# Expert results added to the residual stream in DRAM by accumulating scatters, instead of rows of z that are gathered up and added later

## The chip, the cores and the metric

The kernel runs on one core of one Trainium2 chip. The metric is device time in microseconds (us). Before the change it is 1237.41 us, the median of three runs (1237.15 to 1238.29). The core's engines are named as in the profile: PE multiplies matrices (PEld loads its weights), DVE and ACT work on vectors, POOL works on vectors more slowly and issues the indirect transfers, SP issues plain transfers. The queues of SP, ACT and POOL are each worked in order, and all their transfers run on the same 16 DMA engines.

## What is computed

Two layers act on a residual stream `x` of 3327 rows of 256 floats. Each layer is a graph step and a mixture of experts, both on the normalized stream, both added to it:

```python
x = x + gnn0(layernorm(x), adj)     # mean over neighbours (adj == 1), then a 256x256 matrix
x = x + ffn0(layernorm(x))          # 16 experts 256->512->256 with silu gate, top 2 per row
x = x + gnn1(layernorm(x), adj)     # attention over neighbours (adj != 0), leaky relu
x = x + ffn1(layernorm(x))          # 6 experts 256->256->256->256 with relu, top 2 per row
```

In both mixtures a row's result is the weighted sum over its two best experts, so that each row of `x` gets two added rows per layer. The two experts of one row always differ.

## The kernel before, in words

**Tiles.** Rows are cut into 26 tiles of 128 (the last has 127 rows, N = 3327, NP = 3328). `xs` holds the whole residual stream in SBUF, 128 partitions x 26 tiles x 256. Tiles form chunks of four, and chunks form the blocks of the graph step: 3, 2, 1 and 1 chunks.

**Graph step** (`graph`, L416). For each block, all 26 source tiles are streamed: `load_mask` (L373) loads a piece of the transposed adjacency on SP (three buffers) and DVE turns it into a 0/1 mask (L390), and PE multiplies it with `y`, the prepared rows (L475). In the first block `prepare` is called for one group of tiles after another just ahead of its use: groups of 1, 1, 2, then 4 tiles. `prepare0` (L515) loads `x` into `xs` on SP. `prepare1` (L673) first has to bring the first layer's expert results into `xs`. Both then normalize (`norm`, L173, whose power is taken on POOL at L183) and write `y`. A finished block goes through `finish` (L423): `update` adds the result to `xs`, `norm` gives `h`, SP stores `h` to `hd` in DRAM (L439), and `after` computes the routing. `dispatch` (L192) writes for each row and each of its two experts an entry of three words to the expert's list in DRAM, by a scatter on POOL (L265): where the result is to go, which row of `hd` to read, and the weight.

**Experts.** An expert's list is worked in slots: 67 slots of 128 rows in layer 0, 31 of 256 rows in layer 1. SP loads the slot's list entries (`places`, L320, tile `who`), POOL gathers the rows from `hd` (`rows_in`, L328, one indirect transfer per 128 rows), PE turns them and multiplies (L626, L641 in layer 0, L737, L747 in layer 1), DVE applies bias and weight (L643, L750, L752), and POOL scatters the rows (`rows_out`, L350). The slots are software pipelined by hand: in layer 1 the gathers of slot s + 3 are issued ahead of the scatters of slot s - 1, in layer 0 those of s + 2. The weights of an expert are loaded on SP when a slot begins another expert. Slots are not full: the lists are first filled with idle entries (tile `idle`, L165) whose target lies out of bounds, and the scatter leaves such rows out.

**The results.** A scatter goes to `zd`, which has two rows of 256 for every row of `x`, one for each of its two experts. No two scatters write the same row, so `zd` is declared as disjoint views (L94) and no scatter waits for another. `results` (L362) loads z for a chunk on SP. In layer 1's `prepare1` the two z rows are added on POOL (on DVE for the first chunk, L678) and the sum is added to `xs` on DVE (L679). At the end of the kernel all z is loaded again, added to `xs` on DVE (L777) and stored from ACT's queue (L779, and L784 for the 127 rows of the last tile).

Halfway through layer 0's experts ACT's queue packs the weights of layer 1's experts into one DRAM array, `w1d`, by transfers from DRAM to DRAM (`pack1`, L604).

Of the kernel before, what the change touches and what calls it, by code (L numbers as in the profile page):

```python
# [9 lines left out]
F32 = mybir.dt.float32  # L10
I32 = mybir.dt.int32
# [4 lines left out]
OP = mybir.AluOpType  # L16
# [3 lines left out]
P = 128  # L20
# [5 lines left out]
def kernel(  # L26
# [26 lines left out]
    nc = tc.nc  # L53
    N, D = x.shape
    E0, _, H0 = ffn0_w1.shape
# [18 lines left out]
    SLOTS0 = (2 * N - E0) // P + E0  # L74
    S1 = 2 * P
    SLOTS1 = (2 * N - E1) // S1 + E1
    FAR = 1 << 20
# [12 lines left out]
        dram.tile([E * NP + 2 * P, 3], I32, name=f"list{i}") for i, E in enumerate((E0, E1))  # L90
    ]
    views = [dram_disjoint_views(li[:, :], 2 * NT) for li in lists]
    zd = dram.tile([2 * NP, D], F32, name="zd")
    zviews = dram_disjoint_views(zd[:, :], max(SLOTS0, 2 * SLOTS1))  # L94
    def row_bc(v, name):
        n = v.shape[0]
        t = const.tile([P, n], F32, name=name)
# [36 lines left out]
    slot_p1 = slot_numbers("slot_p1", S1, 3)  # L134

    where = const.tile([P, NT, 2, 3], I32, name="where")
    nc.gpsimd.iota(where, pattern=[[2 * P, NT], [1, 2], [0, 3]], base=0, channel_multiplier=2)
    nc.gpsimd.iota(where[:, :, :, 1], pattern=[[P, NT], [0, 2]], base=0, channel_multiplier=1)
    where_w = where.bitcast(F32)[:, :, :, 2]

    none = const.tile([P, 1], F32, name="none")
# [6 lines left out]
    def operands():  # L148

        small["w0"] = by_chunk(gnn0_wt, "w0t"), row_bc(gnn0_wt[DL, :], "w0r")  # L150
        small["w1"] = by_chunk(gnn1_w, "w1t"), row_bc(gnn1_w[DL, :], "w1r")
        small["gw"], small["gb"] = by_chunk(gate_w, "gw"), row_bc(gate_b, "gb")
        small["a"] = row_bc(gnn1_a[D:], "a_bc")
        small["rw1"] = by_chunk(router_w1, "rw1")
        small["rb1"] = const.tile([P, 1], F32, name="rb1")
        nc.scalar.dma_start(small["rb1"], router_b1.rearrange("(p o) -> p o", o=1))
        small["rw2"] = const.tile([P, E1], F32, name="rw2")
        nc.scalar.dma_start(small["rw2"], router_w2)
        small["rb2"] = row_bc(router_b2, "rb2")
        for li in lists:  # L160
            nc.scalar.dma_start(li.rearrange("(p c) w -> p c w", p=P), idle[:, : li.shape[0] // P, :])
        if N < NP:
            nc.scalar.dma_start(zd[2 * N :, :], zrow[: 2 * (NP - N), :])

    idle = const.tile([P, (E0 * NP + 2 * P) // P, 3], I32, name="idle")  # L165
    nc.gpsimd.memset(idle, 0)
    nc.gpsimd.memset(idle[:, :, 0], FAR)
    zrow = const.tile([2, D], F32, name="zrow")
    nc.gpsimd.memset(zrow, 0.0)

    last = {}
# [175 lines left out]
        nc.scalar.copy(xT, ps)  # L347
        return xT

    def rows_out(s, who, y):  # L350
        n = who.shape[1]
        for h in range(n):
            nc.gpsimd.indirect_dma_start(  # L353
                out=zviews[n * s + h], out_offset=bass.IndirectOffsetOnAxis(ap=who[:, h, 0:1], axis=0),
                in_=y[:, h, :], in_offset=None, bounds_check=2 * NP - 1, oob_is_err=False,
            )

    def weight(who, h):

        return who.bitcast(F32)[:, h, 2:3]  # L360

    def results(blk, zp):  # L362

        n, t0 = len(blk), blk[0]
        z = zp.tile([P, BT, 2, D], F32, name="z")
        nc.sync.dma_start(z[:, :n], zd[2 * t0 * P : 2 * (t0 + n) * P, :].rearrange("(t p k) d -> p t k d", p=P, k=2))
        return z

# [47 lines left out]
    def graph(name, prepare, value, op, wx, update, after, steps, between=None):  # L416
        with ExitStack() as st:
# [5 lines left out]
            def finish(blk, aT):  # L423

                n, t0 = len(blk), blk[0]
                for i, t in enumerate(blk):
                    r = rows(t)
                    ps = ps_mm.tile([P, D + 1], F32, name="mm")
                    for k in range(KD):
                        nc.tensor.matmul(ps[:r], aT[:, k, i * P : i * P + r], wx[:, k, :],  # L430
                                         start=(k == 0), stop=(k == KD - 1))
                    rden = work.tile([P, 1], F32, name="rden", bufs=4)
                    nc.vector.reciprocal(rden[:r], ps[:r, D:])
                    update(t, r, ps, rden)
# [12 lines left out]
                yield  # L447
                yield from after(blk, hT)
# [3 lines left out]
            for b, block in enumerate(GRAPH):  # L452
# [30 lines left out]
                parts = []  # L483
# [153 lines left out]
    def out0(s, who, hid):  # L637
        w3 = w0[s % 2][2]
        ps = ps_acc.tile([P, 512], F32, name="acc")
        for c in range(NC0):  # L640
            nc.tensor.matmul(ps[:, :D], hid[:, c, :], w3[:, c // 2, c % 2, :], start=(c == 0), stop=(c == NC0 - 1))  # L641
        y = io.tile([P, 1, D], F32, name="y")
        nc.vector.tensor_scalar(y[:, 0, :], ps[:, :D], weight(who, 0), None, op0=OP.mult)  # L643
        rows_out(s, who, y)

    who, xg, xT, hid, which = {}, {}, {}, {}, {}
    for s in range(-3, SLOTS0 + 1):
# [19 lines left out]
    stage.close()  # L667


    stage = ctx.enter_context(ExitStack())  # L670
    zp = stage.enter_context(tc.tile_pool(name="zp", bufs=2))

    def prepare1(y, g):  # L673
        n = len(g)
        z = results(g, zp)
        for i, t in enumerate(g):
            adder = nc.vector if t < BT else nc.gpsimd
            adder.tensor_tensor(z[:, i, 0, :], z[:, i, 0, :], z[:, i, 1, :], op=OP.add)  # L678
            nc.vector.tensor_tensor(xs[:, t, :], xs[:, t, :], z[:, i, 0, :], op=OP.add)  # L679
        h = norm(g)  # L680
        er = work.tile([P, BT], F32, name="er")
        for i in range(n):
            prod = work.tile([P, D], F32, name="er_prod", bufs=1)
            nc.vector.scalar_tensor_tensor(prod, h[:, i, :], 1.0, wx["a"], op0=OP.mult, op1=OP.mult,
                                           accum_out=er[:, i : i + 1])
        w = work.tile([P, BT], F32, name="w")
        nc.scalar.activation(w[:, :n], er[:, :n], AF.Exp, bias=wx["c"])
        cols = y[:, g[0] : g[-1] + 1, :, :]
        nc.scalar.copy(cols[:, :, 0, DL], w[:, :n])
        nc.vector.tensor_tensor(cols[:, :, 1, DL], w[:, :n], cols[:, :, 0, DL].bitcast(F32), op=OP.subtract)  # L690
        for i, t in enumerate(g):
            nc.scalar.activation(y[:, t, 0, :DL], h[:, i, :DL], AF.Copy, scale=w[:, i : i + 1])  # L692
            nc.vector.scalar_tensor_tensor(y[:, t, 1, :DL], h[:, i, :DL], w[:, i : i + 1],
                                           y[:, t, 0, :DL].bitcast(F32), op0=OP.mult, op1=OP.subtract)
# [20 lines left out]
        yield  # L715

    graph("1", prepare1, 0.0, OP.not_equal, wx[1], update1, after1, 8)
    stage.close()


    NC1 = H1 // P
# [20 lines left out]
    def out1(s, who, h2):  # L742
# [10 lines left out]
        rows_out(s, who, y)  # L753

    who, xg, xT, h1, h2 = {}, {}, {}, {}, {}
    for s in range(-4, SLOTS1 + 1):
# [12 lines left out]
        if 0 <= s + 2 < SLOTS1:  # L769
            xT[s + 2] = turned(xg.pop(s + 2))  # L770

    tail = ctx.enter_context(tc.tile_pool(name="tail", bufs=len(CHUNKS)))
    zs = [results(blk, tail) for blk in CHUNKS]
    for blk, z in zip(CHUNKS, zs):
        for i, t in enumerate(blk):
            for k in range(2):
                nc.vector.tensor_tensor(xs[:, t, :], xs[:, t, :], z[:, i, k, :], op=OP.add)  # L777
# [42 lines left out]
```

## Time and profile before

| | |
|---|---|
| median of three runs | 1237.41 us |
| profiled execution, its own time | 1231.33 us |
| its span, first to last instruction | 1229.5 us |
| PE busy | 1011.1 us (82%) |
| DVE busy | 457.8 us (37%) |
| ACT busy | 273.3 us (22%) |
| POOL busy | 419.2 us (34%) |
| layer 0: graph / experts, about | 12 to 281 / 292 to 703 us |
| layer 1: graph / experts, about | 703 to 994 / 994 to 1193 us |
| sum of z, store of the result | 1193 to 1229.5 us |
| HBM read, written | 263.18 MB, 33.69 MB |

The page's slices cut the span into 40 equal parts of 30.7 us and give the busy share of each engine in tenths. The chain that ended last is read backwards from the last instruction: each step is what released the one after it. A group of instructions has its busy time, the mean of one, and the idle time of the engine just before it with what ended that. In a row of the timeline the square brackets give the idle time ahead of the instruction and its releaser. "To landing" is the time from a transfer's issue to its completion.

### The profile page before, as it was taken

How to read it: one execution, taken by the hardware profiler on the slowest of the kernel's cores; microseconds unless marked ns; L12 is line 12 of the kernel's file. 1: busy time of each engine (PE TensorE's matmuls, PEld its weight loads, DVE VectorE, ACT ScalarE, POOL GpSimd, SP SyncE). 2: the span in 40 equal slices, each digit the busy share in tenths (PEclk: the TensorE clock that was granted, in tenths of full speed). 3: DMA queues.
4: the chain of work that ended last, by engine and by line, in shares of the span. 5: the costliest groups of instructions: out<-in, count | busy, mean ns of one | idle time of the engine just before them, and what ended most of it. 6: DMA issues, size and time to landing. Idle time of an engine off the chain costs nothing. (4 is left out here: it accounts for less than half of the span.)

```text
span 1229.5 us, 18090 instructions
## 1 busy us (share of the span) xinstructions
PE 1011.1 (82%) x5644; PEld 868.0 (71%) x5644; DVE 457.8 (37%) x1527; ACT 273.3 (22%) x580; POOL 419.2 (34%) x436
## 2 busy tenths in 40 slices
PE   5989979643959999999999768999598429999960
PEld 4768756523959999999999746877476218888850
DVE  5555634532211212212122189666165222222215
ACT  2312012011101111111111133231131204444420
POOL 2000323522322333333333252102333355676730
PEclk9989989875989999999999979999799659999995
DMA  8977653235595655666454057975452044645627
GB/s 301 329 264 260 202 188 105 61 106 193 159 287 158 197 187 192 192 198 199 157 188 108 23 205 267 306 277 177 126 156 71 26 127 139 231 130 167 183 69 292
DMA packets 110572, 221.37 MB, mean 180 GB/s; under 512 B 33390, under 2 KB 55408, under 8 KB 110476
## 3 DMA queue, kind: packets, MB, share of 16 engines
q1 hardware_dynamic: 84240, 178.59, 43.5%
q0 software_dynamic: 15712, 30.73, 9.0%
q10 hardware_dynamic: 10524, 10.89, 2.9%
q8 instruction: 45, 0.74, 0.2%
q14 instruction: 51, 0.42, 0.1%
HBM read 263.18 MB, written 33.69 MB: 241 GB/s over the span
## 5 line engine op out<-in xcount | busy, mean ns | idle before, releaser
L475 PE MATMUL acc<-big,y 128*128 128x512 f32 (+3 forms) x1248 | 305.8, 394 | 42.2 <-ACT y L692 18.7
L475 PEld LDWEIGHTS acc<-big,y 128*128 128x128 f32 (+1 forms) x1248 | 228.5, 197 | 99.6 <-ACT y L692 19.9
L626 PE MATMUL mm<-xT,w 128*128 128x128 f32 x2144 | 266.5, 283 | 14.9 <-ACT xT L347 14.9
L626 PEld LDWEIGHTS mm<-xT,w 128*128 128x128 f32 x2144 | 261.3, 199 | 15.1 <-ACT xT L347 15.1
L353 POOL DMA_INDIRECT zd<-y,who x129 | 128.5, 996 | 264.2 <-DVE y L643 221.6
L265 POOL DMA_INDIRECT list<-where,t_idx x104 | 108.7, 1045 | 203.6 <-DVE t_idx L262 48.4
L333 POOL DMA_INDIRECT xg<-hd,who x129 | 125.7, 974 | 93.7 <-issue 39.0
L634 DVE TENSOR_TENSOR hid<-hid,mm 128x512 f32<-128x512 f32 x67 | 46.0, 687 | 266.5 <-PE mm L626 251.4
L390 DVE TENSOR_SCALAR big<-adj 128x1536 fp32r<-128x1536 int32 (+5 forms) x112 | 107.9, 966 | 95.5 <-PE acc L475 70.1
L641 PE MATMUL acc<-w,hid 128*128 128x256 f32 x536 | 126.6, 379 | 0.0
L188 ACT ACTIVATE ln_h<-xs,ln_nmr,ln_rstd 128x256 f32<-128x256 f32 x104 | 54.4, 591 | 246.0 <-DVE ln_nmr L185 231.7
L641 PEld LDWEIGHTS acc<-w,hid 128*128 128x128 f32 x536 | 96.7, 190 | 10.4
L347 ACT COPY xT<-mm 128x256 f32<-128x256 f32 (+1 forms) x98 | 43.1, 440 | 273.7 <-PE mm L345 248.8
L183 POOL TENSOR_TENSOR ln_rstd<-ln_rstd,half 128x4 f32<-128x4 f32 (+2 forms) x32 | 31.9, 999 | 184.4 <-DVE ln_rstd L182 94.1
L738 ACT ACTIVATE h<-mm,v 128x256 f32<-128x256 f32 x124 | 58.7, 473 | 100.3 <-PE mm L737 100.3
L750 DVE TENSOR_TENSOR y<-acc,v 128x512 f32<-128x512 f32 x31 | 21.4, 691 | 155.6 <-PE acc L747 155.6
L445 PE MATMUL mm<-ident,ln_h 128*128 128x128 f32 x104 | 24.3, 351 | 63.3 <-ACT ln_h L188 63.1
L345 PE MATMUL mm<-ident,xg 128*128 128x128 f32 x258 | 47.7, 286 | 33.8 <-DMA xg<-hd,who 33.8
L345 PEld LDWEIGHTS mm<-ident,xg 128*128 128x128 f32 x258 | 45.7, 199 | 40.5 <-issue 30.0
L737 PE MATMUL mm<-xT,v 128*128 128x256 f32 x248 | 65.9, 389 | 0.7 <-ACT xT L347 0.7
L737 PE MATMUL mm<-h,v 128*128 128x256 f32 x248 | 64.1, 380 | 1.3 <-ACT h L738 1.1
L445 PEld LDWEIGHTS mm<-ident,ln_h 128*128 128x128 f32 x104 | 14.9, 169 | 70.4 <-ACT ln_h L188 69.4
(158 smaller groups left out, 940.4 us busy)
## 6 DMA issues: line engine op xcount, KB each, us to landing
w<-in_ffn_w SPq DMA_DIRECT2D x201, 512.0 KB
adj<-in_adj_t SPq DMA_DIRECT2D x50, 768.0 KB
adj<-in_adj_t SPq DMA_DIRECT2D x36, 1024.0 KB
v<-w1d SPq DMA_DIRECT2D x31, 898.0 KB
z<-zd SPq DMA_DIRECT2D x11, 1024.0 KB
hd<-ln_h SPq DMA_DIRECT2D x12, 512.0 KB
adj<-in_adj_t SPq DMA_DIRECT2D x12, 510.0 KB
w1d<-in_ffn_w ACTq DMA_DIRECT2D x3, 1536.0 KB
```

The lines of the kernel that those rows point to most:

```text
L188: last["h"] = nc.scalar.activation(h[:, i, :], xs[:, t, :], AF.Identity, bias=nmr[:, i : i + 1], scale=rstd[:, i : i + 1])
L265: nc.gpsimd.indirect_dma_start(out=rows_of[2 * (t0 + j) + i], out_offset=bass.IndirectOffsetOnAxis(ap=idx[:, i, j : j + 1], axis=0), in_=w ...
L333: nc.gpsimd.indirect_dma_start(out=xg[:, h, :], out_offset=None, in_=hd, in_offset=bass.IndirectOffsetOnAxis(ap=who[:, h, 1:2], axis=0),)
L345: nc.tensor.transpose(ps[:, k, h * P : (h + 1) * P], xg[:, h, k:D:KD], ident)
L353: nc.gpsimd.indirect_dma_start(out=zviews[n * s + h], out_offset=bass.IndirectOffsetOnAxis(ap=who[:, h, 0:1], axis=0), in_=y[:, h, :], in_ ...
L390: nc.vector.tensor_scalar(mask[:kr, :, :cols], a[:kr, :, :cols], value, None, op0=op)
L475: nc.tensor.matmul(acc[c][k][:, :w], y[:kr, j, part, k * P : (k + 1) * P], mask[:kr, jj, i0 : i0 + w], start=(j == 0 and part == 0), stop= ...
L626: nc.tensor.matmul(q[:, c, :], w[:, k, h0 : h0 + 2 * P - 1 : 2], xT[:, k, :], start=(k == 0), stop=(k == KD - 1))
L634: nc.vector.tensor_mul(hid, hid, ps[1])
L641: nc.tensor.matmul(ps[:, :D], hid[:, c, :], w3[:, c // 2, c % 2, :], start=(c == 0), stop=(c == NC0 - 1))
L737: nc.tensor.matmul(ps[:, c, :], w[:, k, c : H1 : NC1], src[:, k, :], start=(k == 0), stop=(k == 1))
L738: nc.scalar.activation(dst[:, c, :], ps[:, c, :], AF.Relu, bias=w1s[s % 3][:, BB + 2 * i + c : BB + 2 * i + c + 1])
```

## The change

`zd` is gone. A new DRAM array `xd` holds the residual stream, NP rows and 256 rows more. After each graph step's update, SP stores the chunk of `xs` to `xd` (`store`, just ahead of the store of `h`). Each expert slot adds its rows to `xd` by a scatter with an add as its compute operation. The list entry's target is now the row itself, the same for both experts. Since two slots can now add to the same row, a slot's scatters wait until those of the slot before have landed; only the two scatters of one slot in layer 1 are declared free of each other. An idle entry can't be left out by its bounds: it points to one of the 256 spare rows, distinct within a slot. `prepare1` loads `xs` from `xd` in one plain load per group, and there is nothing to add. At the end the result is copied from `xd` to the output by four transfers from DRAM to DRAM, in turn on SP and ACT.

```diff
-    zd = dram.tile([2 * NP, D], F32, name="zd")
-    zviews = dram_disjoint_views(zd[:, :], max(SLOTS0, 2 * SLOTS1))
+    xd = dram.tile([NP + S1, D], F32, name="xd")
...
-    nc.gpsimd.iota(where, pattern=[[2 * P, NT], [1, 2], [0, 3]], base=0, channel_multiplier=2)
-    nc.gpsimd.iota(where[:, :, :, 1], pattern=[[P, NT], [0, 2]], base=0, channel_multiplier=1)
+    nc.gpsimd.iota(where, pattern=[[P, NT], [0, 2], [0, 3]], base=0, channel_multiplier=1)
...
-            nc.scalar.dma_start(zd[2 * N :, :], zrow[: 2 * (NP - N), :])
+            nc.scalar.dma_start(xd[N:NP, :], zrow[: NP - N, :])
+        for h in range(S1 // P):
+            nc.scalar.dma_start(xd[NP + h * P : NP + (h + 1) * P, :], zrow)
...
-    idle = const.tile([P, (E0 * NP + 2 * P) // P, 3], I32, name="idle")
-    nc.gpsimd.memset(idle, 0)
-    nc.gpsimd.memset(idle[:, :, 0], FAR)
-    zrow = const.tile([2, D], F32, name="zrow")
+    idle = {}
+    for i, li in enumerate(lists):
+        n = li.shape[0] // P
+        idle[n] = const.tile([P, n, 3], I32, name=f"idle{i}")
+        nc.gpsimd.memset(idle[n], 0)
+        at = idle[n][:, :, 0]
+        nc.gpsimd.iota(at, pattern=[[1, n]], base=0, channel_multiplier=n)
+        nc.vector.tensor_scalar(at, at, S1 - 1, None, op0=OP.bitwise_and)
+        nc.vector.tensor_scalar(at, at, NP, None, op0=OP.add)
+    zrow = const.tile([P, D], F32, name="zrow")
...
-    def rows_out(s, who, y):
-        n = who.shape[1]
-        for h in range(n):
-            nc.gpsimd.indirect_dma_start(
-                out=zviews[n * s + h], out_offset=bass.IndirectOffsetOnAxis(ap=who[:, h, 0:1], axis=0),
-                in_=y[:, h, :], in_offset=None, bounds_check=2 * NP - 1, oob_is_err=False,
-            )
+    def rows_out(who, y):
+        those = []
+        for h in range(who.shape[1]):
+            ins = nc.gpsimd.indirect_dma_start(
+                out=xd[:, :], out_offset=bass.IndirectOffsetOnAxis(ap=who[:, h, 0:1], axis=0),
+                in_=y[:, h, :], in_offset=None, compute_op=OP.add,
+            ).ins
+            for other in those:
+                tc.declare_no_dep(ins, other, reason="no row twice in a slot")
+            those.append(ins)
...
-    def results(blk, zp):
+    def stream(blk):
         n, t0 = len(blk), blk[0]
-        z = zp.tile([P, BT, 2, D], F32, name="z")
-        nc.sync.dma_start(z[:, :n], zd[2 * t0 * P : 2 * (t0 + n) * P, :].rearrange("(t p k) d -> p t k d", p=P, k=2))
-        return z
+        return xd[t0 * P : (t0 + n) * P, :].rearrange("(t p) d -> p t d", p=P), xs[:, t0 : t0 + n, :]
...
+    def store(blk):
+        to, x_ = stream([t for t in blk if t < NF])
+        nc.sync.dma_start(to, x_)
+        if blk[-1] >= NF:
+            nc.sync.dma_start(xd[NF * P : N, :], xs[: N - NF * P, NF, :])
...
                 h = norm(blk)
+                store(blk)
                 nc.sync.dma_start(hd[t0 * P : (t0 + n) * P, :].rearrange("(t p) d -> p t d", p=P), h[:, :n, :])
...
     def prepare1(y, g):
         n = len(g)
-        z = results(g, zp)
-        for i, t in enumerate(g):
-            adder = nc.vector if t < BT else nc.gpsimd
-            adder.tensor_tensor(z[:, i, 0, :], z[:, i, 0, :], z[:, i, 1, :], op=OP.add)
-            nc.vector.tensor_tensor(xs[:, t, :], xs[:, t, :], z[:, i, 0, :], op=OP.add)
+        of, x_ = stream(g)
+        nc.sync.dma_start(x_, of)
         h = norm(g)
...
-    tail = ctx.enter_context(tc.tile_pool(name="tail", bufs=len(CHUNKS)))
-    zs = [results(blk, tail) for blk in CHUNKS]
-    for blk, z in zip(CHUNKS, zs):
-        for i, t in enumerate(blk):
-            for k in range(2):
-                nc.vector.tensor_tensor(xs[:, t, :], xs[:, t, :], z[:, i, k, :], op=OP.add)
-        full = [t for t in blk if t < NF]
-        nc.scalar.dma_start(
-            out[full[0] * P : (full[-1] + 1) * P, :].rearrange("(t p) d -> p t d", p=P),
-            xs[:, full[0] : full[-1] + 1, :],
-        )
-        if blk[-1] >= NF:
-            nc.scalar.dma_start(out[NF * P :, :], xs[: N - NF * P, NF, :])
+    parts = 4
+    of, to = (a.rearrange("n d -> (n d)").rearrange("(q p f) -> q p f", q=parts, p=N * D // N // parts)
+              for a in (xd[:N, :], out))
+    for q in range(parts):
+        (nc.sync, nc.scalar)[q % 2].dma_start(to[q], of[q])
```

More of the change, by code (lines that the diff above doesn't have):

```diff
@@ L160, in operands @@
         for li in lists:
-            nc.scalar.dma_start(li.rearrange("(p c) w -> p c w", p=P), idle[:, : li.shape[0] // P, :])
+            nc.scalar.dma_start(li.rearrange("(p c) w -> p c w", p=P), idle[li.shape[0] // P])
         if N < NP:
-            nc.scalar.dma_start(zd[2 * N :, :], zrow[: 2 * (NP - N), :])
-    idle = const.tile([P, (E0 * NP + 2 * P) // P, 3], I32, name="idle")
-    nc.gpsimd.memset(idle, 0)
-    nc.gpsimd.memset(idle[:, :, 0], FAR)
-    zrow = const.tile([2, D], F32, name="zrow")
+            nc.scalar.dma_start(xd[N:NP, :], zrow[: NP - N, :])
[11 more added lines that the diff above has]
+    zrow = const.tile([P, D], F32, name="zrow")
     nc.gpsimd.memset(zrow, 0.0)
@@ L643, in out0 @@
         nc.vector.tensor_scalar(y[:, 0, :], ps[:, :D], weight(who, 0), None, op0=OP.mult)
-        rows_out(s, who, y)
+        rows_out(who, y)
     who, xg, xT, hid, which = {}, {}, {}, {}, {}
@@ L667 @@
     stage.close()
-    stage = ctx.enter_context(ExitStack())
-    zp = stage.enter_context(tc.tile_pool(name="zp", bufs=2))
     def prepare1(y, g):
         n = len(g)
-        z = results(g, zp)
-        for i, t in enumerate(g):
-            adder = nc.vector if t < BT else nc.gpsimd
-            adder.tensor_tensor(z[:, i, 0, :], z[:, i, 0, :], z[:, i, 1, :], op=OP.add)
-            nc.vector.tensor_tensor(xs[:, t, :], xs[:, t, :], z[:, i, 0, :], op=OP.add)
+        of, x_ = stream(g)
+        nc.sync.dma_start(x_, of)
         h = norm(g)
@@ L717 @@
     graph("1", prepare1, 0.0, OP.not_equal, wx[1], update1, after1, 8)
-    stage.close()
     NC1 = H1 // P
@@ L752, in out1 @@
             nc.vector.tensor_scalar(y[:, h, :], y[:, h, :], weight(who, h), None, op0=OP.mult)
-        rows_out(s, who, y)
+        rows_out(who, y)
     who, xg, xT, h1, h2 = {}, {}, {}, {}, {}
```

## The prediction, made before the result was known

> **What bounds the kernel now.** I read the page's busy table and slices first, then the chain that ended last, then busy time by windows at the stages that the change touches, and last the POOL rows of the expert loops.
>
> ```profile
> span 1229.5 us, 18090 instructions
> PE   5989979643959999999999768999598429999960
> POOL 2000323522322333333333252102333355676730
> ```
>
> PE is near full from slice 9 to 21 (layer 0's experts) and 34 to 38 (layer 1's). The holes are the ends of stages: slice 22 to 24 (start of layer 1's graph) and the last one. POOL is at half or more in layer 1's experts. The end of the chain, in order of time (start, length, what):
>
> ```profile
> 1189.79 0.97 POOL zd L353
> 1190.76 0.30 POOLq L816
> 1191.07 2.12 DMA zd<-y,who
> 1193.25 5.28 DMA z<-zd
> 1198.54 17.41 DMA z<-zd
> 1215.98 3.77 DVE xs L777 x11
> ```
>
> From the last scatter's landing at 1193.2 everything to 1229.5 is tail: 36.3 us. Busy time by windows (PE, PEld, DVE, ACT, POOL, then granted clock, DMA share, GB/s) shows how it is spent:
>
> ```profile
> 1206.00:1210.00 4.00, 0.00 (x0) 0.00 (x0) 3.40 (x12) 0.00 (x0) 0.00 (x0) 0.50 1.07 401
> 1222.00:1226.00 4.00, 0.00 (x0) 0.00 (x0) 0.00 (x0) 0.00 (x0) 0.00 (x0) 0.50 0.06 19
> 1226.00:1229.50 3.50, 0.00 (x0) 0.00 (x0) 0.00 (x0) 0.00 (x0) 0.00 (x0) 0.50 0.04 15
> ```
>
> The DMA engines are full with 6.8 MB of z and the stores behind it until about 1221. Then one engine in sixteen (share 0.06) works for 6 us: the last store, the 127 rows of tile 25. The start of layer 1's graph, by windows and by PE's waits in its first block:
>
> ```profile
> 712.00:760.00 48.00, 37.29 (x134) 28.68 (x135) 43.11 (x121) 15.53 (x38) 22.16 (x24) 0.86 0.68 233
> ```
>
> ```profile
> PE acc L475 <- ACT y L692: 18.7, 3, 12.1
> PE acc L475 <- DVE big L390: 2.6, 1, 2.6
> ```
>
> DVE is busy 43.1 of 48 us, PE idles 10.7, and most of that is waiting for y, which waits for z and its adds. The scatters, as groups (busy, mean ns | idle before, ended by) and as rows of layer 1:
>
> ```profile
> L353 POOL DMA_INDIRECT zd<-y,who x129 | 128.5, 996 | 264.2 <-DVE y L643 221.6
> L333 POOL DMA_INDIRECT xg<-hd,who x129 | 125.7, 974 | 93.7 <-issue 39.0
> ```
>
> ```profile
> 1029.40 1.01 POOL L353 DMA_INDIRECT zd<-y,who  x1 [0.31 <-issue]
> 1030.71 0.98 POOL L353 DMA_INDIRECT zd<-y,who  x1 [0.30 <-issue]
> 1032.00 1.03 POOL L333 DMA_INDIRECT xg<-hd,who  x1 [0.30 <-PE mm L737]
> 1033.34 0.97 POOL L333 DMA_INDIRECT xg<-hd,who  x1 [0.31 <-issue]
> 1034.61 1.01 POOL L353 DMA_INDIRECT zd<-y,who  x1 [0.30 <-issue]
> ```
>
> No scatter waits for another today. A layer 1 slot is two gathers and two scatters, 5.2 us of POOL back to back against PE's 5.68 (3.48 + 0.47 + 1.73 in the chain). In layer 0 it is one of each, 2.6 against 5.72.
>
> **The change, part by part.** The sum is against the profiled execution, 1231.33 us with a span of 1229.5; the median of the runs shown is 1237.41, 6.1 or 0.5% above, and I put the difference on that.
>
> *Tail.* Gone: 6.8 MB of z loads, 52 adds, 3.4 MB of stores, the one-engine store. New: four copies of 0.85 MB, half on SP and half on ACT, 3.41 MB. The nearest row is the DRAM to DRAM packing of w1d: from 354 to 366 us, DMA share 1.02 to 1.05, 334, 315 and 306 GB/s. At their mean, 318, the copy takes 10.7 us; it could take 8.5 (the 400 GB/s of the z loads) or 17 (every byte paid twice at 400). Its 64 rows per copy divide over sixteen engines, unlike 127. First bytes: z was issued at 1193.25 and its first window, 1194 to 1198, has a share of 0.84, so bytes flow from 1194.6, 1.4 us later. After the last byte: share 0.04 in the last 3.5 us is one engine for 2.2 of them, leaving 1.3. So the end is 1193.2 + 0.7 (the scatter's later landing, below) + 1.4 + 10.7 + 1.3 = 1207.3: **-22.2 us** (-24.4 to -15.9).
>
> *The scatter itself.* Two unknowns, since no row accumulates. Its POOL time: no less than a plain scatter, 1.00, and no more than a gather of the old rows and a scatter, 0.97 + 1.00 = 1.97. Payload does not move it (list scatters of 12 bytes a row take 1.05), and 128 indices are what it shares with the row of 1.00, so I take 1.00. Its landing: now 2.4 to 3.1, median 2.8 from issue; a gather, which also fetches from DRAM, has 3.5, and a gather and a scatter in turn 6.3. The one difference that the trace gives between fetching from and writing to DRAM is 3.5 - 2.8 = 0.7, so I add 0.7 (0 to 3.5). Dummy rows now land too (8576 rows against 6654 real ones); the issue never shrank with skipped rows (971 to 1017 ns), so 0.
>
> *The new wait.* A slot's first scatter waits for the slot before to land. Behind it on POOL stand the next gathers, and PE waits for those. Layer 0: scatter to scatter 5.72, landing 2.8 + 0.7 = 3.5: nothing, up to a landing of 5.7. Layer 1: from the second scatter to the next first are 3.90 back to back (1030.71 to 1034.61), landing 3.5: nothing, up to 4.3, where the slot is 1.3 + 4.3 = 5.6 and PE no longer hides it. **0.**
>
> [...]
>
> *Layer 0 to layer 1.* The last two scatters of layer 0 start at 698.82 and 700.55. The last now waits: 698.82 + 2.47 + 0.7 = 702.0, and lands at 705.2 instead of 703.0, +2.2. After it a 128 KB load instead of 256 (0.4 less at 300 GB/s) and DVE's three adds in the path (706.01 to 707.15, and 0.34 later) are gone: **+0.3** until PE's first matmul.
>
> *Layer 1's first block.* Gone: 26 residual adds and 4 z adds on DVE (14.4 + 1.6 us), 22 z adds on POOL (19.5), half of 6.8 MB, and SP's waits for a free z buffer. What is late next is adj: 20.4 + 3.4 MB in 71 us of PE work is 337 GB/s, about what the engines reach. PE took 88.0 us from first matmul to the block's end, 10.7 idle. The twin is layer 0's first block, which loads x plainly, as will now be done: 84.6 us. So -3.4 to -10.7, and I take the middle: **-7**.
>
> *New stores of x.* Seven per layer plus two of 127 rows, each on SP just ahead of the hd store, which waits for later work than they do, so SP only pays 0.4 us each. They lie in stages with a DMA share of 0.41 to 0.68. The 127 rows take some 7 us on one engine, as in the tail, and can hold the hd store behind them to about 983; the first gather comes at 1000. **0**; without that cover, +7 twice.
>
> *Start.* POOL: one more memset of 474 (about 0.4) and two iotas of 418 and 158 (where's of 156 took 0.61: 1.6 and 0.6), less 0.64 and 0.25. The first rstd is ready at 6.1 and used at 10.6, so that hides. DVE gets four operations on these, about 1.7, hidden only if they fall in its idle time before 9.15. ACT stores 257 KB more while DMA is at 0.92: 0.8. **+1** (0 to 3).
>
> *Layer 0's stall at 355 to 370* (PE waits 14.9 while w1d is packed and DMA is full): two or three slots' extra 128 KB at 310 GB/s, **+1** (0 to 5).
>
> Sum: -22.2 + 0 + 0.3 - 7 + 0 + 1 + 1 = -26.9, so 1237.4 - 26.9 = **1210.5 us**. Its own range is 1201 to 1219.
>
> **The rivals.** *Slower: the accumulating scatter makes POOL the bound of layer 1.* At an issue of 1.97 the slot is 2 x 1.27 + 2 x 2.27 = 7.1 us against 5.68. With 26 slots before the gathers end, that is +37: 1248. It decides from a slot of 5.68 + 26.9/26 = 6.7, an issue of 1.8 or a landing of 5.4 after the second scatter. At the far end, a landing of 6.3, the slot is 7.6 (+50), layer 0's 6.3 (66 x 0.58 = +38): about 1300. For it: POOL has the least room of all queues there. Against: the rows do not scale with bytes.
>
> *Half of that:* a slot of 5.9 to 6.5 takes back 6 to 21 us: 1217 to 1232.
>
> *No gain:* the tail is hidden anyway? Nothing lies beside it: PE has no work after 1188. Only copies at a third of the rate (32 us) would undo it; this with a slot of 5.9 ends within 0.2%, which is about what a measurement of this kernel can tell from no change.
>
> **How the numbers follow.** Forecast 0.50; half 0.18; slower 0.29; no difference 0.03. So faster 0.68, same 0.03, slower 0.29. The range runs from 1203, leaving a tenth below, to 1258, past the slot of 7.1, leaving a tenth above.
>
> **What would show it.** Last scatter to end about 15 us, no share of 0.06; POOL rows at 1.0 us with waits for the previous slot under 0.3; PE idle below 6 in layer 1's first block; layer 1's slots still 5.68. Scatter rows of 1.3 or more, or POOL waiting on xd in the expert loops, would prove me wrong.

## The result, and the profile after

The changed kernel takes 1252.43 us, the median of four runs (1249.97 to 1258.44), against 1237.85 us for the kernel before on the same chip: a ratio of 1.0119 (95% interval 1.0075 to 1.0164). It is slower by 14.6 us where I forecast 26.9 us less. Its profiled execution took 1258.44 us (span 1256.6), the slowest of the four, so that some 6 us of what follows belong to that one execution. The profiled execution of the kernel before was 6 us below its own median, so that the two profiles lie 27 us apart and not 14.6. A second profile of the changed kernel, on another chip, is set beside them.

The page's span and slices of the changed kernel, then two of its costliest groups (busy, mean ns | idle before, ended by):

```profile
span 1256.6 us, 17814 instructions
PE   5989979634949999999999769996995279989870
POOL 3000323522423444444444310005115357677752
...
L361 POOL DMA_INDIRECT xd<-y,who x129 | 203.3, 1576 | 266.1 <-DMA xd<-y,who 90.1
L340 POOL DMA_INDIRECT xg<-hd,who x129 | 128.1, 993 | 72.9 <-issue 28.6
```

The same 129 scatters take 1576 ns of POOL each, not 996, while the gathers are nearly as they were (993 and 974). And what holds the scatters up longest is now an earlier scatter's landing (90.1 us in all), where it was DVE's `y`.

The stages, from the starts of the scatters, of PE's first matmul of layer 1's graph and of the end of its first block, in us. The third column is a second execution of the changed kernel, of 1246.09 us (`r1_after` below):

| stage | before | after | after, second profile |
|---|---|---|---|
| start to the first scatter of layer 0 | 310.5 | 313.8 | 312.5 |
| layer 0: first scatter to the last but one | 388.3 | 400.9 | 390.9 |
| to the last one | 1.7 | 4.5 | 4.6 |
| to PE's first matmul of layer 1's graph | 11.3 | 13.0 | 12.8 |
| layer 1's first block | 88.0 | 73.2 | 73.2 |
| to layer 1's first scatter | 221.0 | 222.1 | 221.6 |
| layer 1: first to last scatter | 170.2 | 211.6 | 211.4 |
| last scatter to the end | 38.4 | 17.4 | 17.4 |

The two ends that the change was made for gain what was hoped or more: 21.0 us at the end, 14.8 in the first block. Layer 1's expert stage loses 41.4 (41.2 in the second profile), more than both. The rest is layer 0, where the two executions differ: 12.6 us lost in the one, 2.6 in the other. The column before is low in its first two rows: three more profiles below, of kernels with plain scatters in layer 0 and the packing as it was (`e4_layer1_only`, `e5_split_store`, `e6_no_z_adds`), take 312.3 to 313.3 us for the first row and 390.7 to 391.3 for the second. Beside them the second profile's layer 0 loses nothing between the first scatter and the last but one, and the first profile's 10.

The end, by rows of the timeline (start, length, what, in brackets the idle time before) and by windows (PE, PEld, DVE, ACT, POOL, then granted clock, DMA share, GB/s):

```profile
1239.15 1.55 POOL L361 DMA_INDIRECT xd<-y,who  x1 [0.30 <-issue]
1243.02 1.44 SPq L785 DMA_DIRECT2D out_x<-xd  x2
```

```profile
1246.00:1250.00 4.00, 0.00 (x0) 0.00 (x0) 0.00 (x0) 0.00 (x0) 0.00 (x0) 0.50 1.14 413
1250.00:1254.00 4.00, 0.00 (x0) 0.00 (x0) 0.00 (x0) 0.00 (x0) 0.00 (x0) 0.50 0.73 226
1254.00:1256.60 2.60, 0.00 (x0) 0.00 (x0) 0.00 (x0) 0.00 (x0) 0.00 (x0) 0.50 0.00 0
```

The last scatter lands 3.9 us after its start, at 1243.0; from there to 1256.6 are 13.6 us where there were 36.3. No window has the share of one engine in sixteen any more. Layer 1's first block, a window that answers to the one of before:

```profile
732.00:780.00 48.00, 47.49 (x192) 37.80 (x192) 41.98 (x153) 26.21 (x66) 7.08 (x7) 0.93 0.71 231
```

PE is busy in 47.5 of 48 us, with 192 matmuls in place of 134, and the granted clock is 0.93, not 0.86. The rows of POOL in layer 1's experts:

```profile
1124.61 1.01 POOL L340 DMA_INDIRECT xg<-hd,who  x1 [0.30 <-PE acc L756]
1125.93 0.98 POOL L340 DMA_INDIRECT xg<-hd,who  x1 [0.30 <-issue]
1128.05 1.62 POOL L361 DMA_INDIRECT xd<-y,who  x1 [1.14 <-DMA xd<-y,who]
1129.97 1.57 POOL L361 DMA_INDIRECT xd<-y,who  x1 [0.30 <-issue]
1131.85 1.01 POOL L340 DMA_INDIRECT xg<-hd,who  x1 [0.30 <-issue]
```

A slot is two gathers of 1.30 (with the 0.3 between instructions) and two scatters of 1.88: 6.4 us of POOL back to back, where it was 5.2 and PE's 5.68 set the pace. On top of that the slot's first scatter waits for the second one of the slot before; in this slot POOL idles 1.14 us ahead of it.

### The profile page after: what moved, and what is told of

It is laid out like the page before. It is cut to its first block, busy times and chain, and to the rows that moved or that the text cites. A ratio compares the mean times of both kernels' runs of the same rounds, so it can differ in the third digit from the quotient of the medians.

```text
span 1256.6 us, 17814 instructions
## 1 busy us (share of the span) xinstructions
PE 1019.3 (81%) x5644; PEld 867.8 (69%) x5644; DVE 421.6 (34%) x1449; ACT 272.9 (22%) x580; POOL 475.8 (38%) x415
## 5 line engine op out<-in xcount | busy, mean ns | idle before, releaser
L361 POOL DMA_INDIRECT xd<-y,who x129 | 203.3, 1576 | 266.1 <-DMA xd<-y,who 90.1
L352 PE MATMUL mm<-ident,xg 128*128 128x128 f32 x258 | 52.0, 296 | 50.5 <-DMA xg<-hd,who 50.2
```

Source lines behind the costliest of these rows:

```text
L352: nc.tensor.transpose(ps[:, k, h * P : (h + 1) * P], xg[:, h, k:D:KD], ident)
L361: ins = nc.gpsimd.indirect_dma_start(out=xd[:, :], out_offset=bass.IndirectOffsetOnAxis(ap=who[:, h, 0:1], axis=0), in_=y[:, h, :], in_off ...
```

## The experiments

Four theories of where the loss comes from, as the expectations name them. **A**, a chain of landings: a slot's scatters wait until those of the slot before have landed, and an accumulating scatter lands late. **B**, issue: POOL needs 1.57 us for a scatter that adds and 1.00 for one that doesn't, and POOL becomes the bound of layer 1. **C**: any wait between scatters would do it, whatever they compute. **D**: the idle rows, which were left out before and now all land on 256 spare rows. A and B are two halves of my "slower" rival. The runs were made on several chips, and each is compared only with the kernel before on its own chip: 1239.23 us for the first four, 1238.71 for `r1_after`, `r2_skip_idle`, `e6_no_z_adds` and `r3_before_spread`, about 1270 for the others.

**The add alone taken away.** The waits, the spare rows, the stores of x, the plain load and the copy at the end all stay.

```diff
-                in_=y[:, h, :], in_offset=None, compute_op=OP.add,
+                in_=y[:, h, :], in_offset=None,
```

> The changed kernel with the add taken out of the scatter: same target rows, same waits between slots, but a plain write (so the sums are not formed: a row keeps one writer's data). Theory A (the chain of landings: each slot waits for the landing of the slot before, and an accumulating landing takes 4.5 to 8 us where a plain one took 2.8): landing falls back to about 2.8, slots to 5.68 in layer 1 and 5.72 in layer 0, so 1252 - 41 (layer 1) - 13 (layer 0) - 3 = about 1196, 1190 to 1212. Theory B (the longer issue on POOL, 1.57 us for 1.00): the same time, since the issue falls back too. Theory C (a wait on any scatter costs that much, whatever it does): 1240 or more, slots of layer 1 near 7.

Measured: 1202.74 us, ratio 0.9714 (0.9673 to 0.9755). The transfers of `xd` in this kernel (duration ns min/median/max, first and last start) and their landings, then the same of the changed kernel:

```profile
L361 POOL DMA_INDIRECT xd<-y,who x129: 962/978/1004, 311.5 to 1181.6; - x129
...
DMA to landing us min/median/max: 2.4/2.5/10.8
```

```profile
L361 POOL DMA_INDIRECT xd<-y,who x129: 1538/1566/1689, 313.8 to 1239.2; - x129
...
DMA to landing us min/median/max: 3.6/4.6/10.1
```

A profile gives the landing of some of the scatters only: of 50 in this kernel and of 34 in the changed one. With the same waits and the same spare rows, layer 1's expert stage takes 170.3 us and layer 0's 391.5. So C falls: a wait behind a landing of 2.5 us costs next to nothing (1.4 us between the last two scatters of layer 0), and plain writes to the spare rows don't cost either. What is left of D, adds to these rows, is tested below. By the ratios the add itself is worth 50 us, or 43 with that of `r1_after`. Without it the rest of the change gains 36.5 us, more than the 26.9 of my forecast.

**The wait relaxed.** Two copies of the residual stream in DRAM, even slots add to the one and odd slots to the other, so that a slot waits for the one before the last. Only the first copy is read, so half of the sums are left out. The line that matters:

```diff
-                out=xd[:, :], out_offset=bass.IndirectOffsetOnAxis(ap=who[:, h, 0:1], axis=0),
+                out=(xd, xe)[s % 2][:, :], out_offset=bass.IndirectOffsetOnAxis(ap=who[:, h, 0:1], axis=0),
```

> The changed kernel with two copies of the residual array, both stored after each graph step; slots add in turn to the one and the other, so a slot waits for the slot before the last one. Only the first copy is used afterwards (the sums of every other slot are left out). Adding and its issue are unchanged. Theory A: the wait is off the path, layer 1's slot is what POOL's issues make of it, 2 x 1.3 + 2 x 1.9 = 6.4 while there are gathers and 5.68 after them, 190 us from first to last scatter instead of 210; layer 0 goes back to 5.72 and loses its 10 us; 1252 - 18 - 12 = about 1222, 1215 to 1232. Theory B: the issue is nearly all of it, layer 1 stays within 5 us of 210 and the time within 1242 to 1252. The added 6.8 MB of stores lie in the graph steps and should cost 0 to 2.

Measured: 1219.35 us, ratio 0.9848 (0.9809 to 0.9886), with the store of the second copy in it. POOL's rows in layer 1's experts:

```profile
1103.33 1.00 POOL L343 DMA_INDIRECT xg<-hd,who  x1 [0.30 <-PE mm L355]
1104.63 0.98 POOL L343 DMA_INDIRECT xg<-hd,who  x1 [0.30 <-issue]
1105.92 1.62 POOL L364 DMA_INDIRECT xd<-y,who  x1 [0.30 <-issue]
1107.84 1.58 POOL L364 DMA_INDIRECT xd<-y,who  x1 [0.30 <-issue]
1109.72 1.00 POOL L343 DMA_INDIRECT xg<-hd,who  x1 [0.30 <-PE mm L355]
```

Here POOL never waits, and the slot is 1109.72 - 1103.33 = 6.39 us, slot after slot. That is B alone. Layer 1's 30 slots then split as follows, from the scatters' starts: the first 25, with gathers, take 144.0 us before, 162.6 with issue alone, 177.8 in the changed kernel; the last five, without gathers, 25.0, 20.6 and 32.0. Issue alone is worth 18.6 - 4.4 = 14 us of layer 1's loss, the landings 15.3 + 11.4 = 27. In the last five slots POOL has time enough, and the slot is still 6.4: 1.85 for the first scatter and some 4.5 until the second has landed and POOL starts again. Layer 0 is at 391.5, as with plain scatters: there the longer issue costs nothing, and what layer 0 loses comes from the landings.

**One layer at a time.** Accumulating scatters in layer 0 only, with z rows and the old end in layer 1; and the other way round (`ACC` is then the reverse, and the other call is replaced). `rows_out_z` is the `rows_out` of before.

```diff
+    ACC = (True, False)
...
-        rows_out(who, y)
+        rows_out_z(s, who, y)
```

> Accumulating scatters and the plain load of x in layer 0 and the step after it, z rows and the old end in layer 1. From the two profiles, layer 0's part is: first scatter 3.3 later, slots +12.6, last two scatters and the load +4.5, first block of layer 1's graph -14.9. Sum +5.5: 1243, 1236 to 1250. If the slots' loss is only the profiled execution's (the slowest of four), it ends at 1233 to 1238.

> Z rows in layer 0, accumulating scatters and the copy at the end in layer 1. From the profiles: first to last scatter 210 instead of 170 us (+40), last scatter to the end 17.4 instead of 38.4 (-21), so +19: 1257, 1247 to 1262. If the parts are independent, the distance of this one and of the layer 0 one from the kernel before add up to that of the whole change, 14.6.

Measured: 1231.45 us in layer 0 only, ratio 0.9937 (0.9914 to 0.9959), and 1261.46 in layer 1 only, 1.0186 (1.0141 to 1.0231). The gain of 7.8 and the loss of 22.2 make 14.4, as much as the whole change cost in its first runs (14.6), while in `r1_after` below it cost 7.8. Whether the halves interact by a few us is not settled by this. I had expected 1243 for layer 0 alone and was 12 us too high, below even my case of a loss that only the profiled execution had (1233 to 1238), because I worked from the profile of the changed kernel. The execution profiled here is again the slowest, 1240.39 us, with the same 400.9 us of layer 0. One more of the ten took 1238.90, the other eight 1228.00 to 1232.86, so the long stage looks like something that only some executions fall into.

**The changed kernel once more, and its idle rows left out again** (their target out of bounds, the bounds given to the scatter, which then does leave them out, with 30.74 MB on POOL's queue in `e7_skip_idle` and 34.00 in the changed kernel: the description of the change is wrong in saying that it can't).

```diff
-        nc.vector.tensor_scalar(at, at, NP, None, op0=OP.add)
+        nc.vector.tensor_scalar(at, at, FAR, None, op0=OP.add)
...
-                in_=y[:, h, :], in_offset=None, compute_op=OP.add,
+                in_=y[:, h, :], in_offset=None, compute_op=OP.add, bounds_check=NP + S1 - 1, oob_is_err=False,
```

> The changed kernel itself once more, beside the kernel before. The loss so far: 1.012 of the kernel before where that kernel's layer 1 expert stage takes 170 us (first to last scatter). Where it takes 200 us, as in one call, PE and not the scatters sets the slot. Theory A (chain of landings) and B (issue) both have the changed kernel's stage at 209 to 214 us whatever the stage before takes, since POOL and the landings set it: ratio 1.010 to 1.015 beside a stage of 170, 0.980 to 0.990 beside one of 200. If the accumulating scatters merely add to whatever PE takes, the stage would be 40 us longer than before in both, and the ratio 1.012 in both.

> The changed kernel whose idle entries are left out by their bounds again, so that 6654 rows are added per layer and not some 8576 or 7936. Beside the changed kernel on the same chip: theory A with a landing that grows with the rows expects the landings 0.3 to 1 us shorter and the time 5 to 15 us shorter, most of it in layer 0 (a quarter of whose rows are idle); theory B expects no difference of the time, within 3 us, because an issue costs the same with any number of rows; theory D (the idle rows all land on 256 spare rows, and are what is slow) expects layer 1's stage back below 190 us and some 30 us less.

Measured on one chip: 1246.53 us, ratio 1.0058 (1.0033 to 1.0084), and 1239.93, ratio 1.0025 (0.9999 to 1.0050). The loss is there again, half as large; below the range that I had given. The stage table shows why it can be: layer 1 lost the same 41 us, layer 0 lost 2.6 us in place of 12.6. The scatters of the first, then of the second:

```profile
L361 POOL DMA_INDIRECT xd<-y,who x129: 1538/1566/1637, 312.5 to 1226.9; - x129
...
DMA to landing us min/median/max: 3.6/3.9/8.6
```

```profile
L361 POOL DMA_INDIRECT xd<-y,who x129: 1538/1566/1681, 313.1 to 1220.7; - x129
...
DMA to landing us min/median/max: 2.7/3.9/11.9
```

Leaving the idle rows out is worth 6.6 us: layer 1 took 207.7 instead of 211.4, and the landings begin at 2.7 us rather than 3.6, with the same median of 3.9. Layer 0, where I had expected most of the gain, took 391.4 instead of 390.9 up to its last scatter but one. So theory D is at most a small part, and the scatter's issue does not shrink with rows left out: its median stays at 1566 ns. The same kernel was first run on a chip where the kernel before takes 1270 us:

> The changed kernel with idle entries pointing out of bounds again, so that the accumulating scatter leaves them out (8576 rows fall to 6654 in layer 0, 7936 to 6654 in layer 1). Theory A (the chain of landings): most slots are full and land as before, only those with idle rows land sooner: first to last scatter of layer 1 within 5 us of 211, time 1244 to 1253. Rival D (the 256 spare rows, hit by slot after slot, are what makes the landing long): landing falls to 3.5 or less, the time to 1235 or below.

Measured there: 1249.40, ratio 0.9839 (0.9787 to 0.9892), so that on that chip the same kernel is faster than the one before. The windows of layer 1's expert stage say why: the kernel before in its own profile, then on that chip (the kernel of `e5_split_store`, which has the same stage), columns as above:

```profile
1020.00:1190.00 170.00, 167.70 (x822) 146.54 (x820) 41.23 (x93) 72.23 (x146) 110.90 (x113) 1.00 0.50 157
```

```profile
1020.00:1220.00 200.00, 181.29 (x826) 153.31 (x825) 38.59 (x87) 72.81 (x149) 109.21 (x111) 0.94 0.45 139
```

The same 820 or so matmuls take PE 181 us there, at a granted clock of 0.94, with gaps of 19 us. Over all the profiles, layer 1's expert stage with plain scatters is 170 to 173 us on some of the chips and 196 to 200 on two others (granted clock 0.94 to 0.98); why, the profiles don't tell. With accumulating scatters that wait for the slot before it is 208 to 214 on all of them. So POOL and the landings set it, not PE, and what the change costs in this stage is the difference to whatever it would have taken.

**The first block's gain.** The kernel before, z loaded as it was, but z added to one column of 256 only and the add of the two z rows left out.

```diff
-            adder = nc.vector if t < BT else nc.gpsimd
-            adder.tensor_tensor(z[:, i, 0, :], z[:, i, 0, :], z[:, i, 1, :], op=OP.add)
-            nc.vector.tensor_tensor(xs[:, t, :], xs[:, t, :], z[:, i, 0, :], op=OP.add)
+            nc.vector.tensor_tensor(xs[:, t, 0:1], xs[:, t, 0:1], z[:, i, 0, 0:1], op=OP.add)
```

> The kernel before; layer 1's first block loads z as before, but the adds of the two z rows are left out, and z is added to the residual stream in one column only (so that the load is still waited for). It tells what the 14.9 us came from that the changed kernel gains in layer 1's first block (88.0 to 73.1 us in the profiles), where I had predicted 7. If it is the adds on DVE and POOL, the block takes 73 to 76 us here and the time falls by 12 to 15 us, ratio 0.988 to 0.990; if it is the 3.4 MB fewer bytes, the block stays at 84 to 88 us and the time within 4 us of the kernel before; in between, both have a part.

Measured: 1224.98 us, ratio 0.9879 (0.9849 to 0.9909), 13.7 us less. Its window:

```profile
716.00:764.00 48.00, 45.28 (x188) 36.67 (x189) 39.83 (x155) 20.38 (x50) 6.36 (x6) 0.95 0.90 314
```

The block takes 74.4 us with all of z's bytes still loaded, at a DMA share of 0.90. So nearly all of the gain is the adds, with the z buffers that they kept occupied (9.0 us of waits of SP's loads of z for the adds to `xs`, in the kernel before), and not the 3.4 MB, to which at most 1.2 of the 14.8 us are left. What DVE's adds and what POOL's cost is not separated; in the kernel before an add of two z rows takes 0.42 us on DVE and 0.90 on POOL at the median. Over the whole block PE idles 10.7 us before, 0.4 in the changed kernel and 2.7 here; its busy time falls from 77.3 to 72.8 and 71.7 for the same matmuls (303 or 304), while the granted clock goes from 0.91 to 0.96.

**Other ways to gain.** The store of the 127 rows as two of 112 and 15; with it, the packing of `w1d` in six transfers of 0.77 MB, eight slots apart, in place of three at once at slot 8 of the 67 (not halfway, as the description of the kernel has it); and accumulating scatters in layer 0 on top of both. `pack1_w` packs one half of one of the three weights, `pack1` then only the small rest.

```diff
-            nc.scalar.dma_start(out[NF * P :, :], xs[: N - NF * P, NF, :])
+            for lo, hi in ((0, 112), (112, N - NF * P)):
+                nc.scalar.dma_start(out[NF * P + lo : NF * P + hi, :], xs[lo:hi, NF, :])
```

```diff
...
+        if s >= 6 and s % 8 == 6 and s // 8 < 6:
+            with tc.issue_after(silu.ins):
+                pack1_w(s // 8)
-        if s == 8:
+        if s == 54:
             with tc.issue_after(silu.ins):
                 pack1()
```

> The kernel before with its last store of 127 rows cut into 112 and 15. If those 127 rows go out through one DMA engine for some 7 us after all else, as the share of 0.06 in the last windows says, and the two pieces spread over more, the end comes 5 to 7 us sooner: 1232 to 1234 beside 1239 for the kernel before. If the last microseconds are something else, no change.

> The kernel before with the split last store, and the packing of layer 1's weights cut into six transfers of 0.77 MB that are issued eight slots apart instead of all at once. If PE's wait of 14.9 us at 355 to 370 is the DMA engines being full with it, most of it goes: 1239 - 6 - 8 to 14 = 1219 to 1225.

> The kernel before with its last store of 127 rows as two of 112 and 15, and the packing of layer 1's weights in six transfers eight slots apart instead of three at once. In an earlier call it took 0.980 of the kernel before: 5 us from the split store and 17 to 20 us from layer 0's stall. If both are worth the same here: 0.978 to 0.984, and 20 to 35 us below the changed kernel beside a layer 1 stage of 170 us.

> Accumulating scatters in layer 0 alone, z rows in layer 1, with the split last store and the spread packing. If layer 0's half of the change keeps its -7.8 beside these: 1231.5 - 6 - 8 to 14 = 1211 to 1218, under the one without it by about 8. If the spread packing lengthens landings in more slots than the packing in one go did, the two end level at 1219 to 1225.

Measured: the split store 1265.00, ratio 0.9970 (0.9944 to 0.9995), 5.3 us. The spread packing with it 1245.35, ratio 0.9797 (0.9759 to 0.9836), and on the chip of `r1_after` 1215.82, ratio 0.9803 (0.9774 to 0.9831): 22.9 us less than the kernel before and 30.7 less than the changed kernel, with plain scatters throughout. Layer 0's stage falls to 375.7 us there, from 390.7 in `e6_no_z_adds` on the same chip. The first of the two gained more than I had expected (24.9 us, not 14 to 20). With accumulating scatters in layer 0, 1247.13, ratio 0.9822 (0.9787 to 0.9858), level with the kernel without them, as I had expected if the landings take the gain back: the first block gains its 14 us and layer 0's stage loses them (386.1 against 373.7, and the last scatters).

**Layer 0's loss.** The changed kernel with the packing spread, and the last kernel once more.

> The changed kernel with the packing of layer 1's weights in six transfers eight slots apart. Theory A (chain of landings) expects the landings beside a transfer of 0.77 MB still to be long, so that the stage of layer 0's experts takes 380 to 386 us, where the kernel before with spread packing has 375.7; the gain over the changed kernel is then 5 to 10 us, ratio to the kernel before 0.998 to 1.004. If the wait costs layer 0 nothing outside the stall, the stage takes 375 to 377 us and the ratio is 0.990 to 0.995. Layer 1's expert stage stays at 211 us in both.

> Accumulating scatters in layer 0 only (layer 1 by z rows as before), the last store in two parts and the packing spread out. Layer 0's half alone gave 0.994, the spread packing with the split store 0.980. If they add: 0.973 to 0.976. If the landings eat the gain of the spread packing (theory A in layer 0): 0.979 to 0.985, level with the kernel before that only has the packing spread, as it was on a slower chip.

Measured: 1250.95, ratio 0.9848 (0.9813 to 0.9883), and 1252.39, ratio 0.9870 (0.9836 to 0.9903), again on a chip where the kernel before takes 1270 us. That the first ratio lies below both of my ranges says nothing of layer 0, since they were meant for a chip with a stage of 170; the second lies above both of its own. The stages do: 393.6 and 391.0 us of layer 0, where the same kernel as the second took 386.1 on the other slow chip and plain scatters 373.7. That is a loss of 12 to 20 us, more than theory A expected, and little or nothing is left of the gain of the spread packing. PE's wait of 15 to 18 us behind the packing in one go is gone in these profiles; instead PE waits 9 to 12 us for gathers, which stand behind late scatters on POOL's queue, where it waits for none with plain scatters. So the loss of layer 0 is not the packing stall alone. Rows of the first profile of the changed kernel, well behind the packing, show what happens:

```profile
444.19 1.56 POOL L361 DMA_INDIRECT xd<-y,who  x1 [4.94 <-issue]
...
448.65 1.57 POOL L361 DMA_INDIRECT xd<-y,who  x1 [1.58 <-DMA xd<-y,who]
...
455.80 1.56 POOL L361 DMA_INDIRECT xd<-y,who  x1 [4.25 <-DMA xd<-y,who]
...
462.94 1.57 POOL L361 DMA_INDIRECT xd<-y,who  x1 [4.26 <-DMA xd<-y,who]
```

Slots of 4.46, 7.15 and 7.14 us. No slot of layer 0 in the changed kernel's two profiles is shorter than 4.4 us, the landing and the restart of POOL (some 0.7 us from a landing to the scatter that waited for it), where plain scatters follow each other at 2.6 in two slots of `b2_before_spread`. So a slot that is late is caught up with slowly, and a landing of over 5 us makes the next one late again. In this execution the 42 slots from 436.4 us on take 250.6 us, 10.4 more than at 5.72 each, and that is all of the difference to the second profile, where the same 42 take 240.4. What decides between the two in one execution I have not settled.

## Why the prediction was wrong

My "slower" rival is what happened: 1248 by its price, 1252.4 and 1246.5 measured. I had given it 0.29. That its price lies so close is partly luck: its slot of 7.1 us came from an issue of 1.97 alone, the measured one of 7.05 from an issue of 1.57 and the landings together, and what layer 1's first block gained beyond my term made up for part of the losses that I hadn't priced. The steps that failed are the scatter's issue and the new wait that I put at nothing: layer 1's expert stage lost 41.4 us, 14 of them by the issue alone and 27 by the landings (`e2_two_targets`). By the steps of the forecast:

- **Tail, -22.2:** right. From the last scatter to the end it measured -21.0; the scatter's landing took 3.9 us where I had 2.8. Behind the landing 13.6 us passed where I had 13.4, but by two errors that cancel: the copy was faster than the 10.7 us that I took from the packing (413 GB/s in one window, and the last byte before 1254), and at least 2.6 us, not 1.3, followed its last byte.
- **The scatter's issue, taken as 1.00 within 1.00 to 1.97:** this step failed. It measured 1.57, worth 14 us of layer 1. "Payload does not move it" and "128 indices are what it shares with the row of 1.00" were both true of the plain rows (1.05 us at 12 bytes a row, 1.00 at 1 KB), and neither said anything of an add. Of the two ends I took the one that was nearest in kind, when nothing in the trace shared the one thing that was new.
- **Landing, +0.7 within 0 to 3.5:** +1.8 in the first profile (2.8 to 4.6), +1.1 in the second (3.9), and up to 10.1 beside the packing. My 2.8 was thin: the profile of before gives the landing of only two of its 129 scatters, at 2.4 and 3.15 us. Without the add the median was 2.5 (50 landings, and 10.8 beside the packing), which makes it +1.4 to +2.1. The bounds held the median and not the spread; a chain pays for the late ones.
- **The new wait, 0:** failed with the two before it. My thresholds were an issue of 1.8 alone or a landing of 5.4 alone. Neither was reached by the medians: 1.57 and about 4.5 together made a slot of 7.05 us, 41.4 us in all where I had 0. The longer issue alone makes 6.4 us of POOL's work in a slot, more than PE's 5.68. A slot's second scatter and the two gathers behind it cover 4.5 us of the landing, and a landing of 3.9 with POOL's restart, some 0.7 us for which I had no term, already takes 4.6. For unknowns on one path the thresholds have to be worked out together.
- **Layer 1's first block, -7 within -3.4 to -10.7:** the sign right, the size half. It measured -14.8, beyond my bound, because I held PE's busy time fixed and bounded the gain by its idle time of 10.7. With the idle time gone the clock granted was higher (0.96, not 0.91), and the same matmuls took 4.5 us less. The twin, layer 0's first block, was no help, and the bytes of adj, which I named as late next, did not hold it back: 311 GB/s with all of z in the kernel without the adds. Of the wait for `y` that I showed, 12.1 of the 18.7 us lay ahead of the block's first matmul.
- **Layer 0 to layer 1, +0.3:** +4.5 from the last scatter but one to PE's first matmul. The last scatter starts 4.5 us after the one before it where I had 3.2, and the rest of the path, where I saved 1.9 us of loads and adds, got 1.7 longer.
- **New stores of x, 0:** from layer 1's first block to its first scatter +1.1 and +0.6, which holds seven of them; nothing to speak of.
- **Start +1, layer 0's stall +1:** the start took 3.3 and 2.0 us to the first scatter, and layer 0's stage 12.6 and 2.6; the bounds held in one execution and not in the other. Beside the other profiles with plain scatters, which start 1.8 to 2.7 us later than the one of before, the start's loss is 1.5 us at most.

The other terms would have made a faster kernel: with the add taken out of the scatter and nothing else changed, 36.5 us. The add made the issue on POOL 0.59 us longer per 128 rows (0.98 to 1.57), and the landing, counted from the same start, 1.4 us later at the median (2.5 without the add, 3.9 in the kernel with two copies, on one chip); what takes the time in the issue, no run here shows. If the landing moves with the issue's end, some two fifths of the later landing are the longer issue itself; no run separates them.

## What to carry to other kernels

The scatter that adds cost twice here: POOL's issue grew from 0.98 to 1.57 us per 128 rows, and since two of them may touch one row, a slot was made to wait for the landings of the one before, 3.9 to 4.6 us at the median; no run has the adds of two slots to one array without this wait. It lost 22 us in layer 1, where gathers and scatters nearly filled the slot already (5.2 of 5.68 us). It gained 7.8 in layer 0, where a slot of 5.72 us leaves POOL more room, but not beside the spread packing: late landings still ate what the first block gained. Before rebuilding a data path, look at what its cost is made of: 22.9 us could be had with plain scatters, by splitting a store that sits on one DMA engine (a share of 0.06 of the sixteen) and spreading one burst of transfers, and the adds ahead of the first block were worth 13.7, though no run here takes them off these engines and still forms the sums.

## What was not expected of the hardware

- The issue of an indirect scatter took 0.98 to 1.00 us for 128 rows and 1.57 with an add, whether or not the bounds leave out the idle rows, a fifth of all.
- In layer 1's first block less idle time went with less time for PE's own work: 77.3 us for its matmuls with 10.7 idle, at a granted clock of 0.91; 72.8 and 71.7 with 0.4 and 2.7 idle, at 0.96.
- The same kernel's layer 1 expert stage took 170 to 173 us on some chips and 196 to 200 on two others, at a granted clock of 1.00 and of 0.94 to 0.98, so that the change was a loss of 0.6 to 1.2% on the ones, while a variant of it gained 1.6% on one of the others.
